# Two graph layers on one core: layer 1's sums moved next to the products of heads 0 to 3, the next tile's mask moved two steps later

## The chip, the cores and the metric

The kernel runs on one core of a Trainium2 chip. The core has a matrix engine (TensorE, PE in the profile, with its weight loads as PEld), a vector engine (VectorE, DVE), a scalar engine (ScalarE, ACT), a general one (GpSimd, POOL) and a queue engine (SyncE, SP) that issues transfers. Each works through its own instructions in order; semaphores tie them together. The metric is the time of one execution on the device in microseconds. The kernel before takes 3070.12 us, the median of three runs (3068.62 to 3073.23).

## The reference

`x` is (16, 1024, 256) in float32, `adj` (16, 1024, 1024) in int32, 0 or 1 with a full diagonal, about one entry in 32 set. Two layers follow each other, both with a normalization first and a residual:

```python
h = maximum(layernorm(x), 0)                       # layer 0: attention with 8 heads of 32
Q, K, V = (h @ W.T + bias for W, bias in ...)      # each split into heads
scores = where(adj == 0, -inf, Q @ K.T * 32**-0.5)
x = x + (softmax(scores) @ V) @ Wo.T + bo

h = maximum(layernorm(x), 0)                       # layer 1: scores by the kind of edge
e_k = leaky_relu((h * a_k) @ h.T, 0.2)             # k = 0..3
scores = where(adj == k + 1, e_k, ...)             # -9e15 where adj is 0
x = x + softmax(scores) @ h
```

With `adj` of 0 and 1, only `e_0` is ever chosen in layer 1; the kernel computes that case and looks at the end whether another kind was seen.

## The kernel before, in words

A *tile* is 128 rows of one of the 16 graphs; a graph has eight (`t` = 0 to 7), so there are 128 tiles. One loop (`for s in range(B * NT + 1)`) runs over them, and in its iteration `s` several tiles are at different stages:

- `now` is tile `s` (class `Attend`): its scores and softmax are made, head by head. `was` is tile `s - 1`: its last two heads, its products, output and residual. `gone` is tile `s - 2`, `nxt` is tile `s + 1`.
- `edge` and `edge_was` are tiles `s - 9` and `s - 10` of layer 1 (class `Edges`): scores and softmax of the one, sums and store of the other. They exist from `s` = 9 and 10 on. The last nine tiles' sums come after the loop.
- `piece` is tile `s + 9` (class `Piece`): its rows are normalized, transposed and projected to q, k and v. It exists up to `s` = 118.

Each iteration has eight *steps*, `h` = 0 to 7, one for each head. The order of the work on every engine is the order of the calls in this loop, written out by hand (`tc.manual_schedule()`); a framework sets the semaphores from the tiles that the instructions read and write. In step `h` the scores of head `h` go to one of two places of 1024 columns (`sides`; heads 4 and 6 to the second, all others to the first, since layer 1 uses the second in steps 0 to 3). DVE adds the mask and finds the row's maximum (`softmax_max`, L473), ACT takes the exponential of the head before (`softmax_exp`, L490), and the head before that is transposed: heads 0, 1, 4 and 5 by DVE in blocks and four transfers from SP (`turn_blocks`, `place_blocks`, L381 and L386), heads 2, 3, 6 and 7 by eight TensorE transposes and two ACT copies (`turn`, L590 and L591). Of tiles with `t` = 7 heads 4 and 5, and of those with `t` = 0 heads 0 and 1, go to TensorE too, with DVE copies; their exponentials write their output in another order.

Four places of 256 columns lie in two banks of the accumulation memory (shown as `acc`): `sums_place` and `brief` in the first, `early` and `late` in the second.

The work that the change touches:

- `combine(0)` in step 7 and `combine(1)` in step 3 of the next iteration: 64 products each (L526), weights of 32 columns, into `sums_place`, four of them beside each other in the array.
- `gather(0)` and `gather(1)`: layer 1's sums, 32 matmuls each (L698), also with 32 columns of weights, 256 columns moving, into `sums_place`. Half 0 ends step 5, half 1 stands in step 6 between the scores and the maximum; `store` behind the maximum divides, adds the residual (L705, L707 on DVE) and issues the output's transfer from SP (L708).
- `residual` of `was` (L547, DVE) reads the output's products (`output`, L541) from `late`; `norms` then takes the statistics of two tiles on DVE (L182, L183) and finishes them on POOL (L167 to L172). Both stand in step 5 ahead of head 5's maximum.
- `piece.turn` in step 5 writes two transposes (L237) to `late`; `piece.turned` copies them out twice on ACT (L249 `hT`, L250 `hTm`); `piece.project(0, ...)`, k's projection, ends step 6: eight matmuls (L267) to `late`; `piece.raised(0)` reads them on ACT in step 7 (L309). q's projection goes to `early` in step 1 and is read in step 4 by `raised(1)` (L309 too); `piece.normed` (L223) follows.
- `nxt.flag` on ACT (L453, squares of `adj - 0.5` with a running sum, in which other kinds of edges show) and `nxt.mask` on POOL (L441) end step 3; both write the mask of the next tile, and the one comes after the other. `nxt2.load` ends step 4: it issues, from POOL, the 512 KB load of the `adj` of the tile after that (L432), into a single buffer that flag and mask must have read.
- On POOL also: `edge.leak` (L674 to L676) and `load_nodes` (L686) in step 3, the split of q and its two transfers in step 4 (L313, L314, L324), `edge_nxt.prepare` (L613), `now.load_nodes` in step 6 (L438), the split of k in step 0.

Of the kernel before, what the change touches and what calls it, by code (L numbers as in the profile page):

```python
# [47 lines left out]
def gnn_kernel(  # L48
# [545 lines left out]
    class Edges:  # L594


        def __init__(self, b, t, last=False):
            self.b, self.t, self.last = b, t, last
            self.rows = slice(t * P, (t + 1) * P)
            self.side = sides[t % 2 if last else 1]  # L600
            self.tags = {"sel": ("p", 4), "pT1": ("pT", 7)} if last else {}
            if last and t % 2:
                self.tags |= {"ha": ("hT", 1), "x1b": ("x1", 1), "h0": ("xb", 1)}
            self.sums = late if last and t % 2 else sums_place

        def buffer(self, tag, shape):
            tag, bufs = self.tags.get(tag, (tag, 1))
# [179 lines left out]
    with tc.manual_schedule():  # L787
        first = [Piece(0, 0, 4), Piece(0, 4, 4)]
        piece_was, piece_next = Piece(1, 0), piece_of(0)
        now, nxt = attend_of(0), attend_of(1)  # L790
# [48 lines left out]
        for s in range(B * NT + 1):  # L839
            b, t = divmod(s, NT)  # L840

            def load_keys(h, end):
                if t == NT - 1 and b + 1 < B and 2 * h + end in KEY_STEPS:
                    load_key(b + 1, KEY_STEPS.index(2 * h + end))
                if t == 0 and 0 < b < B and 2 * (HEADS + h) + end in KEY_STEPS:
                    load_key(b, KEY_STEPS.index(2 * (HEADS + h) + end))

            nxt2, edge_nxt, piece_nxt = attend_of(s + 2), edges_of(s + 1), piece_of(s + 1)
            for h in range(HEADS):
                ending, eh = (now, h - 1) if h >= 1 else (was, HEADS - 1)  # L850
                turning, th = (now, h - 2) if h >= 2 else (was, HEADS + h - 2)

                load_keys(h, 0)


                if now:
                    now.scores(h)
                if h == 0 and piece_was:
                    piece_was.halve(0)
                if s == 0 and h == 1:  # L860
                    first[1].values()
                if h == 3 and edge:
                    edge.softmax_max()
                if h == 5:
                    if was:
                        was.residual()
                    norms(was, piece_nxt)
                if h == 6 and edge_was:
                    edge_was.gather(1)
                if now:  # L870
                    now.softmax_max(h)
                if h == 6 and edge_was:
                    edge_was.store()


                if h == 1 and edge:
                    edge.keep(0)
                if h == 2 and gone:
                    gone.turned_normed()
                if ending:  # L880
                    ending.softmax_exp(eh)

                if h == 3 and was:
                    was.turned_reciprocals()
                if h == 3 and edge:
                    edge.bend()
                    edge.keep(1)


                if h == 3:  # L890
                    if was:
                        was.combine(1)
                    if piece_was:
                        piece_was.biased()
                    if was:
                        was.combined()
                if turning and th in by_blocks(turning.t):
                    turning.turn_blocks(th)
                    turning.place_blocks(th)
                elif turning:  # L900
                    turning.turn(th, 0)
                    turning.turn(th, 1)


                if h == 0:
                    if edge:
                        edge.score(0)
                    if gone:
                        gone.normed()
                    if edge_was:  # L910
                        edge_was.turn_blocks()
                        edge_was.place_blocks()
                if h == 1:
                    if gone:
                        gone.turn_normed()
                    if piece_was:
                        piece_was.project(1, 0)
                        piece_was.project(1, 1)
                    if was:
                        was.reciprocals()  # L920
                    if piece_nxt:
                        piece_nxt.load()
                if h == 2:
                    if edge:
                        edge.score(1)
                    if piece_was:
                        piece_was.values()
                    if was:
                        was.turn_reciprocals()
                        was.add_bias()  # L930
                if h == 3:
                    if nxt:
                        nxt.load_queries()
                    if edge:
                        edge.leak()
                    if edge_was:
                        edge_was.load_nodes()
                    if nxt:
                        nxt.flag()
                        nxt.mask()  # L940
                if h == 4:
                    if was:
                        was.output()
                    if piece_was:
                        piece_was.raised(1)
                        piece_was.halve(1)
                    if piece:
                        piece.normed()
                    if piece_was:
                        piece_was.write_queries()  # L950
                    if edge_nxt:
                        edge_nxt.prepare()
                    if nxt2:
                        nxt2.load()
                if h == 5:
                    if edge_was:
                        edge_was.gather(0)
                    if piece:
                        piece.turn()
                    if piece:  # L960
                        piece.turned()
                if h == 6:
                    if edge:
                        edge.softmax_exp()
                    if was:
                        was.keep()
                    if now:
                        now.load_nodes()
                    if piece:
                        piece.project(0, 0)  # L970
                        piece.project(0, 1)
                if h == 7:
                    if now:
                        now.combine(0)
                    if piece:
                        piece.raised(0)
                load_keys(h, 1)
            gone, was, now, nxt = was, now, nxt, nxt2
            edge_was, edge = edge, edge_nxt
            piece_was, piece = piece, piece_nxt  # L980
# [84 lines left out]
```

## Time and profile before

| what | value |
|---|---|
| median of three runs | 3070.12 us |
| the profiled execution, its own time | 3076.4 us |
| span of its profile | 3074.5 us |
| mean granted TensorE clock | 0.996 |
| ACT, mean of 1024 exponentials (L490) | 1224 ns, and 202 ns for reading the sum |
| DVE, mean of 1024 maxima (L473) | 1208 ns, and 83 ns for reading the result |
| TensorE, layer 1's sums (L698), 8192 matmuls | 496.9 us busy |
| TensorE, the products (L526), 16384 matmuls | 533.4 us busy |
| POOL, mean of 128 masks (L441) | 3655 ns |
| ACT, mean of 128 flags (L453) | 1154 ns, and 196 ns for reading the sum |
| SP and POOL, transfers of `adj` (L432), to landing | 5.0 us |

Busy times of the engines overlap, so they do not add up to the span. A matmul's end is modelled, and matmuls overlap each other; the distance from one start to the next says what a row of them costs. In the timeline a line is a run of like instructions, with its start and its length from the first start to the last end; "idle before" in brackets gives the time that the engine stood still ahead of it and what ended it.

### The profile page before, as it was taken

How to read it: one execution, taken by the hardware profiler on the slowest of the kernel's cores; microseconds unless marked ns; L12 is line 12 of the kernel's file. 1: busy time of each engine (PE TensorE's matmuls, PEld its weight loads, DVE VectorE, ACT ScalarE, POOL GpSimd, SP SyncE). 2: the span in 40 equal slices, each digit the busy share in tenths (PEclk: the TensorE clock that was granted, in tenths of full speed). 3: DMA queues.
4: the chain of work that ended last, by engine and by line, in shares of the span. 5: the costliest groups of instructions: out<-in, count | busy, mean ns of one | idle time of the engine just before them, and what ended most of it. 6: DMA issues, size and time to landing. Idle time of an engine off the chain costs nothing. (4 is left out here: it accounts for less than half of the span.)

```text
span 3074.5 us, 96254 instructions
## 1 busy us (share of the span) xinstructions
PE 2965.6 (96%) x36722; PEld 2230.1 (73%) x36722; DVE 2515.6 (82%) x4453; ACT 2654.5 (86%) x5159; POOL 2177.6 (71%) x2999
## 2 busy tenths in 40 slices
PE   7889999999999999999999999999999999999998
PEld 5667777777777777777777777777777777776664
DVE  5878888888888888888888788888888888888885
ACT  5888888899898998889889888988989888898882
POOL 3657777777777777777777777777777777776542
PEclk9999999999999999999999999999999999999999
DMA  7766777877777786777777777787777777777653
GB/s 245 219 219 205 237 235 222 255 216 243 231 225 243 230 257 209 232 247 220 246 230 228 235 232 243 221 255 221 220 247 228 251 211 235 237 227 236 191 168 100
DMA packets 597828, 695.68 MB, mean 226 GB/s; under 512 B 63280, under 2 KB 528560, under 8 KB 597360
## 3 DMA queue, kind: packets, MB, share of 16 engines
q1 hardware_dynamic: 528288, 477.29, 51.9%
q0 software_dynamic: 66960, 210.04, 21.0%
q8 instruction: 295, 4.83, 0.7%
q10 hardware_dynamic: 2112, 2.10, 0.2%
q14 instruction: 173, 1.42, 0.1%
HBM read 252.98 MB, written 134.22 MB: 126 GB/s over the span
## 5 line engine op out<-in xcount | busy, mean ns | idle before, releaser
L473 DVE CUSTOM_DVE_ANT_0 p<-s,neg 128x1024 f32<-128x1024 f32 x1024 | 1236.2, 1208 | 220.7 <-PE s L461 185.1
L490 ACT ACTIVATE p<-p,nmx 128x1024 f32<-128x1024 f32 x1024 | 1249.4, 1224 | 132.5 <-DVE nmx L473 123.9
L461 PE MATMUL s<-k,qt 128*128 128x512 f32 x2048 | 760.6, 453 | 15.5 <-DVE nmx L473 4.3
L591 ACT COPY pT<-trp 128x512 f32<-128x512 f32 x1024 | 549.4, 590 | 95.3 <-PE trp L590 94.9
L590 PE MATMUL trp<-ident,p 128*128 128x128 f32 x4608 | 604.5, 274 | 4.7 <-ACT pT L591 1.5
L590 PEld LDWEIGHTS trp<-ident,p 128*128 128x128 f32 x4608 | 531.0, 140 | 104.0 <-ACT pT L591 10.8
L381 DVE STREAM_TRANSPOSE blocks<-p 128x1024 f32<-128x1024 f32 x456 | 564.5, 1238 | 12.3 <-ACT p L680 10.6
L526 PE MATMUL acc<-pT,v 128*32 128x128 f32 x16384 | 533.4, 275 | 41.8 <-ACT recT L520 30.0
L526 PEld LDWEIGHTS acc<-pT,v 128*32 128x32 f32 x16384 | 453.5, 110 | 153.0 <-ACT recT L520 85.0
L698 PE MATMUL acc<-h,pT 128*32 128x256 f32 x8192 | 496.9, 382 | 2.8 <-DVE h L707 1.7
L441 POOL TENSOR_SCALAR neg<-adj 128x1024 bf16<-128x1024 int32 x128 | 467.9, 3655 | 42.9 <-ACT neg L453 33.7
L461 PEld LDWEIGHTS s<-k,qt 128*128 128x128 f32 x2048 | 322.9, 191 | 106.3 <-issue 43.0
L698 PEld LDWEIGHTS acc<-h,pT 128*32 128x32 f32 x8192 | 241.8, 109 | 207.8 <-issue 65.6
L676 POOL TENSOR_TENSOR sel<-sel,less 128x1024 f32<-128x1024 f32 x120 | 286.8, 2390 | 68.9 <-ACT less L665 47.6
L633 PE MATMUL s<-h1T,ha 128*128 128x512 f32 (+2 forms) x744 | 272.8, 490 | 2.7 <-ACT h1T L569 1.6
L674 POOL TENSOR_SCALAR less<-top 128x1 f32<-128x1 f32 x120 | 31.9, 266 | 274.0 <-DVE top L656 273.9
L324 POOL DMA_DIRECT2D qd<-halves x240 | 177.5, 780 | 58.7 <-POOL halves L314 31.8
L490 ACT ACTIVATION_READ_ACCUMULATOR p<-p,nmx 128x1 f32 x1024 | 206.8, 202 | 0.0
L510 POOL COPY wide<-rec 128x256 f32<-128x256 f32 x128 | 53.8, 420 | 204.2 <-DVE rec L508 204.2
L330 POOL DMA_DIRECT2D kd<-halves x240 | 172.2, 766 | 35.5 <-POOL halves L314 35.4
L314 POOL TENSOR_TENSOR halves<-full,halves 128x256 fp32r<-128x256 f32 x240 | 176.8, 737 | 20.6
L633 PEld LDWEIGHTS s<-h1T,ha 128*128 128x128 f32 x744 | 126.7, 190 | 70.7 <-issue 45.0
(117 smaller groups left out, 4328.4 us busy)
## 6 DMA issues: line engine op xcount, KB each, us to landing
pT<-blocks SPq DMA_DIRECT2D x2304, 128.0 KB, 3.5
qt<-qd SPq DMA_DIRECT2D x128, 512.0 KB, 4.5
k<-kd SPq DMA_DIRECT2D x128, 512.0 KB, 7.3
adj<-in_adj POOLq DMA_DIRECT2D x127, 512.0 KB, 5.0
qd<-halves POOLq DMA_DIRECT2D x240, 256.0 KB, 2.7
kd<-halves POOLq DMA_DIRECT2D x240, 128.0 KB, 4.1
xb<-in_x POOLq DMA_DIRECT2D x128, 128.0 KB, 4.2
x1d<-x SPq DMA_DIRECT2D x128, 128.0 KB, 4.0
```

The source lines that it names most:

```text
L324: nc.gpsimd.dma_start(out=qds[self.b][self.first, oc].rearrange("p u w n -> p u (w n)"), in_=halves.unsqueeze(1).to_broadcast([P, 2, 2 * P]),)
L381: nc.vector.transpose(blocks.rearrange("p b j q -> p j b q"), p)
L441: nc.gpsimd.tensor_scalar(self.neg, self.adj, 0.0, MASKED, ALU.is_equal, ALU.mult)
L461: nc.tensor.matmul(self.ps[:, cols], lhsT=self.qt[:, h, :], rhs=keysets[self.b][h][:, cols], start=True, stop=True,)
L473: nc.vector.tensor_tensor_reduce(out=p, in0=sides[h in self.second], in1=self.neg, scale=-SCALE, scalar=FLOOR, op0=ALU.add, op1=ALU.min, a ...
L490: nc.scalar.activation(to, of, AF.Exp, bias=nmx, scale=-1.0, accum_out=self.sums[:, h : h + 1])
L526: nc.tensor.matmul(sums_place[r * HD : (r + 1) * HD, g * P : (g + 1) * P], lhsT=vs[self.b][:, j, place_of(h) : place_of(h) + HD], rhs=self ...
L590: nc.tensor.transpose(tr[:, j, :], p[:, jj * P : (jj + 1) * P], ident)
L591: copy(pT[:, half * 4 : half * 4 + 4, :], tr)
L633: nc.tensor.matmul(self.side[:, cols], lhsT=self.ha[:, c, :], rhs=h1T[:, c, cols], start=(c == 0), stop=(c == NC - 1),)
L676: nc.gpsimd.tensor_tensor(self.sel, self.sel, self.less, ALU.subtract)
L698: nc.tensor.matmul(self.sums[a * HD : (a + 1) * HD, :], lhsT=self.pT[:, j, a], rhs=h1s[self.b][:, j, :], start=(j == 0), stop=(j == NT - 1),)
```

## The change

In the loop, five moves; in `Edges.__init__` one place. Layer 1's two half sums and the store leave steps 5 and 6 and stand in step 7 between k's projection, which leaves the end of step 6, and `combine(0)`; inside the loop they use `early` in place of `sums_place`. The maximum of a head is now called ahead of the residual and the norms for all heads (it matters in step 5 alone). Flag and mask of the next tile go from the end of step 3 to the end of step 5, the load of `adj` from the end of step 4 to the start of the second half of step 6. Nothing is added to or taken from the instructions themselves.

```diff
-            self.sums = late if last and t % 2 else sums_place
+            self.sums = (late if t % 2 else sums_place) if last else early
...
                 if h == 3 and edge:
                     edge.softmax_max()
+                if now:
+                    now.softmax_max(h)
                 if h == 5:
                     if was:
                         was.residual()
                     norms(was, piece_nxt)
-                if h == 6 and edge_was:
-                    edge_was.gather(1)
-                if now:
-                    now.softmax_max(h)
-                if h == 6 and edge_was:
-                    edge_was.store()
...
                     if edge_was:
                         edge_was.load_nodes()
-                    if nxt:
-                        nxt.flag()
-                        nxt.mask()
                 if h == 4:
...
                     if edge_nxt:
                         edge_nxt.prepare()
-                    if nxt2:
-                        nxt2.load()
                 if h == 5:
-                    if edge_was:
-                        edge_was.gather(0)
                     if piece:
                         piece.turn()
                     if piece:
                         piece.turned()
+                    if nxt:
+                        nxt.flag()
+                        nxt.mask()
                 if h == 6:
+                    if nxt2:
+                        nxt2.load()
                     if edge:
                         edge.softmax_exp()
...
                     if now:
                         now.load_nodes()
+                if h == 7:
                     if piece:
                         piece.project(0, 0)
                         piece.project(0, 1)
-                if h == 7:
+                    if edge_was:
+                        edge_was.gather(0)
+                        edge_was.gather(1)
+                        edge_was.store()
                     if now:
                         now.combine(0)
```

## The prediction

> **What bounds the kernel now.** I read the busy shares of the page first, then one query tile's period on each engine's timeline, then a few windows. Three engines are near full on the page, and TensorE is fullest:
>
> ```profile
> PE 2965.6 (96%) x36722; PEld 2230.1 (73%) x36722; DVE 2515.6 (82%) x4453; ACT 2654.5 (86%) x5159; POOL 2177.6 (71%) x2999
> ```
>
> A share does not say who sets the pace, so I took TensorE's timeline of one tile, from the scores of head 4 to those of head 0 of the next tile (columns: start, duration, engine, line, what, count):
>
> ```profile
> 1638.65 0.73 PE L461 MATMUL s<-k,qt 128*128 128x512 f32 x2
> ...
> 1640.77 0.81 PE L461 MATMUL s<-k,qt 128*128 128x512 f32 x2
> 1641.42 1.03 PE L590 MATMUL trp<-ident,p 128*128 128x128 f32 x8
> 1642.39 1.93 PE L698 MATMUL acc<-h,pT 128*32 128x256 f32 x32
> 1644.25 0.44 PE L237 MATMUL acc<-ident,h 128*128 128x128 f32 x2
> 1644.45 0.71 PE L461 MATMUL s<-k,qt 128*128 128x512 f32 x2
> 1645.09 1.93 PE L698 MATMUL acc<-h,pT 128*32 128x256 f32 x32
> 1646.96 1.16 PE L267 MATMUL acc<-hT,wkT 128*128 128x128 f32 x8
> 1647.87 0.71 PE L461 MATMUL s<-k,qt 128*128 128x512 f32 x2
> 1648.52 1.96 PE L526 MATMUL acc<-pT,v 128*32 128x128 f32 x64
> 1650.40 0.73 PE L461 MATMUL s<-k,qt 128*128 128x512 f32 x2
> ```
>
> No line shows an idle time, and the stretch is 11.75 us long. I tabulated it over 78 tiles with t from 1 to 6: it lies between 11.73 and 11.76 in every one. So steps 4 to 7 are set by TensorE alone, and that is where the change works. The other engines of the same stretch:
>
> ```profile
> 1642.14 0.42 DVE L547 TENSOR_TENSOR x<-acc,xb 128x256 f32<-128x256 f32 x1 [0.58 <-issue]
> ...
> 1645.20 1.23 DVE L473 CUSTOM_DVE_ANT_0 p<-s,neg 128x1024 f32<-128x1024 f32 x1 [0.32 <-PE s L461]
> ```
>
> ```profile
> 1641.41 0.64 ACT L309 ACTIVATE full<-acc,bq_t 128x128 f32<-128x128 f32 x2
> 1641.92 0.62 ACT L223 ACTIVATE h<-xin,shift,r 128x256 f32<-128x256 f32 x1
> 1642.41 1.16 ACT L490 ACTIVATE p<-p,nmx 128x1024 f32<-128x1024 f32 x1
> 1643.54 1.09 ACT L591 COPY pT<-trp 128x512 f32<-128x512 f32 x2
> 1644.73 0.37 ACT L249 COPY hT<-acc 128x256 f32<-128x256 f32 x1
> 1645.00 0.38 ACT L250 COPY hTm<-acc 128x256 f32<-128x256 f32 x1
> ```
>
> The reader is to see that ACT runs from 1641.41 on with almost no gap, that hTm is done at 1645.38, only 1.6 us before its reader L267, and that the residual L547 stands ahead of head 5's maximum (1643.68, not shown). The two half sums (L698) are what covers these two. In all tiles L547 starts 0.09 us after the second L309 ends or later: both read the bank acc1, one after the other.
>
> **The change on TensorE: what it removes.** Sums between full-array work cost more than their matmuls. The 32 of a half start 1.55 us from first to last (1.93 less one matmul of 0.38), 0.05 each, so 1.60 by themselves, but stand 1.86 to 1.87 apart from what follows: 0.27 to leave. Entering costs 0.09 (transposes to sums 0.97, to L541 0.88; scores to sums 0.64, to transposes 0.57). L267 behind them needs 0.91, elsewhere 0.82. Now the 64 stand in one row with heads 0 to 3's products, both 128x32: one entry, no exit of their own. Step by step, the new row without any wait would be transposes 0.88, L237 0.20, scores 0.56, scores 0.56, L267 0.82 with 0.09 to enter, sums 64 x 0.05 = 3.20, products 1.88: 8.19 instead of 1650.40 - 1641.42 = 8.98. Gain: 0.79 us a tile.
>
> **What the change adds on the path: two waits.** The diff moves head 5's maximum ahead of the residual and the statistics in step 5; only one call moved, but on DVE's queue it changes who waits. L237 writes the place that the residual reads (`late`), so it can't start before it, and the 1.95 us of sums that lay between are gone.
> (a) Head 5's scores end at 1641.58, the maximum starts 0.04 later (as at 1645.20, behind scores that end at 1645.16) and gives DVE free after 1.15; the residual runs 1642.77 to 1643.19; L237 at about 1643.25 (0.06 is what the scores of head 1 need behind a maximum). TensorE is ready at 1641.42 + 0.88 = 1642.30. Wait 0.95.
> (b) L237 0.20, scores 0.56 twice: L267 could start at 1644.57. It needs hTm. ACT without the flag in step 3 starts L309 as soon as the output's products end (1641.13, plus 0.1, which is where L309 stands in the tiles in which ACT is early: 2.57 us after head 4's scores): 1641.22. Then, by the starts above, 0.51 + 0.49 + 1.13, then 0.95 for the copies (1503.81 to 1504.76 in a tile with t = 7), 0.27 and 0.38: hTm at 1644.95. L267 0.07 later, 1645.02. Wait 0.45. So the flag, gone from step 3, buys only 0.2 us here, since ACT then waits for TensorE.
> Sum for a tile: 0.95 + 0.45 - 0.79 = **0.61 us slower**; heads 0 to 3 end at 1651.01.
>
> **Tiles with t = 7** take a third wait. There heads 4 and 5 are transposed on TensorE in steps 6 and 7, and their exponentials, which reorder, take twice as long:
>
> ```profile
> 1505.28 2.26 ACT L490 ACTIVATE p<-p,nmx 128x1024 f32<-128x1024 f32 x1
> ```
>
> That is head 5's, right behind hTm; the next ACT work starts 2.07 later. The flag (L453: 1.15 from its start, 1638.18, to the next) now sits ahead of it: 1505.28 + 1.15 + 2.07 = 1508.50. Head 5's transposes start at 1508.6; TensorE, without the sums before it, is through with head 7's scores near 1506 and waits 2.6 us. Then 0.85 + 0.91 + 3.20 + 1.88 = 1515.4, against 1511.57 before: 3.87 slower.
>
> **A wait also costs clock.** Of the first ten tiles six have a stretch of 3.41 us at half clock, each behind a 3.41 us stretch with 1.69 us or more of idle TensorE; stretches with 1.64 or less did not have it:
>
> ```profile
> 57.66:61.07 3.41, 1.33 (x8) 0.87 (x8) 2.77 (x5) 3.41 (x8) 2.96 (x5) 1.00 0.00 0
> 61.07:64.48 3.41, 3.41 (x33) 2.67 (x36) 1.58 (x4) 2.34 (x6) 3.08 (x8) 0.50 0.76 238
> ```
>
> (PE busy is the first number after the length, the granted clock the third from the end.) The price, from the starts in that tile: L267 to scores 1.40 for 0.91, scores to products 1.13 for 0.65, products 2.48 for 1.88, 1.6 in all. A wait of 2.6 reaches 1.69 in one of two stretches about 8 times in 10. The waits of the other tiles leave TensorE idle for some 1.1 to 1.4 us within one stretch, so none is taken there; at the upper end one tile in six.
> The Trainium skill ("TensorE: Matmul & The Clock Gate", Part 1 and its closing table) asks for an idle window or gap of about 3.4 us before the clock is halved. By that rule a wait of 2.6 us costs no clock and the forecast would be 17 us lower; the rows above show it behind 1.7 us, and I go by them.
>
> **What lies beside other work.** The mask (3.66 us) moves on POOL behind the split of q, its two DMAs, the scaling of the next tile and the norms. POOL by its rows: split from 1641.95, DMAs from 1643.0, scaling 1644.75, norms 1645.7 to 1647.35, mask to 1651.0. Its reader, head 0's maximum of the next tile, waits for scores that end at 1651.87 then: margin 0.85, price nothing; beyond it each us would be paid in full. The load of adj (0.80 to issue, 5.0 to land) is issued at 1651 and needed a period later. On DVE the store waits for the sums (end 1649.5) with nothing behind it but that same maximum; its DMA passes two heads' block moves on SP's queue and has only layer 1's next blocks behind it, which need DVE first. k's evacuation on ACT (L309) now stands behind the store, in one bank, until 1650.5; head 7's exponential is then done near 1651.7, and its transposes come after the next scores of head 1. Head 5's exponential, behind the flag in the other tiles too, ends at 1647.1, and DVE comes to its transposes at 1647.7. All at nothing.
>
> **Sum.** Sums in the loop from s = 10, a piece to project until s = 118: 109 tiles, 13 of them with t = 7. 96 x 0.61 = 59; 13 x 3.87 = 50; clock 13 x 0.8 x 1.6 = 17; s = 119, t = 7 without a piece, +3; the last nine tiles have no piece, hence no wait (a) or (b), and DVE and ACT take part of the gain: -4 (between 0 and -7). The first ten have no sums: 0 (5 either way). Together +125: the profiled span 3074.5 (run 3076.4) becomes 3200; against the median 3070.1, **3195 us**.
>
> **Rivals.**
> 1. The waits stay hidden and the gain is kept. For it: TensorE is the full engine, and 0.79 is solid. It needs (a) and (b) to add to less than 0.79, that is the residual done 0.6 us earlier than DVE's own rows allow. 119 x -0.79 = -94: 2976. Chance 0.04.
> 2. Only (a) binds because ACT is early by half a us, and the flag does not delay head 5: 109 x 0.16 = 17: 3087. Against it: the copies' durations are fixed and their start is set by TensorE. Chance 0.06.
> 3. The mask comes late on POOL. Its margin is 0.85 us; at 1.85 us of delay, from a slower split or contention, a us more on each of 109 tiles: 3304. Chance 0.06.
> 4. The two orders are the same in effect: no change, 3070. Against it: the instruction listings differ as described. Chance 0.02.
>
> The likeliest has 0.82. Range 3140 to 3230: the low end is (a) and (b) together 0.25 shorter, t = 7 at 2.5 and no clock lost (96 x 0.36 + 13 x 2.5 = 67); the high end has 0.15 more a tile and the clock lost in one tile of six (14 + 25). A difference over 0.2% (6 us) can be told from none here: faster 0.04, same 0.02, slower 0.94.
>
> **What would show it.** Right: in the changed trace L237 waits about 0.9 us for DVE's L547, L267 some 0.4 for ACT's L250, the 64 sums run straight into the 64 products, head 4's scores to head 0's take 12.3 us (17 or more for t = 7), and the clock falls in the t = 7 tiles. Wrong: L237 without idle time; head 0's maximum waiting for POOL's L441; or a gap between the sums and the products.

## The result, and the profile after

| | median | lowest to highest | runs |
|---|---|---|---|
| before | 3071.68 us | 3068.62 to 3074.89 | 4 |
| changed | 3241.62 us | 3240.40 to 3244.79 | 4 |

The changed kernel takes 1.0555 times as long, with a 95% interval of 1.0536 to 1.0573: 170 us slower. The forecast was 3195 us within 3140 to 3230. The sign and the causes were right; the amount was 45 us short, and 12 us outside the range. The span of the changed kernel's profile is 3238.5 us against 3074.5, so 164 us have to be found in the trace.

The busy shares of the page first. TensorE does the same 36722 matmuls in nearly the same busy time as before, but the share is 91% instead of 96%: it now waits.

```profile
PE 2954.5 (91%) x36722; PEld 2278.3 (70%) x36722; DVE 2506.4 (77%) x4453; ACT 2661.5 (82%) x5159; POOL 2178.2 (67%) x2999
```

The view of waits says for what. Its columns are the engine with its line, the work it waited for, the total in us, how often, and the longest; three lines of the changed kernel:

```profile
PE acc L237 <- DVE x L547: 104.1, 118, 1.0
...
PE trp L590 <- ACT p L490: 40.1, 18, 2.6
...
PE acc L267 <- ACT hTm L250: 37.7, 106, 1.3
```

These are the forecast's three waits: the transposes of the piece for the residual, head 5's transposes in the tiles with `t` = 7, and k's projection for the second copy. TensorE's timeline of one regular tile, from head 4's scores to the next head 0's, shows where two of them stand:

```profile
1683.23 0.73 PE L461 MATMUL s<-k,qt 128*128 128x512 f32 x2
...
1685.35 0.81 PE L461 MATMUL s<-k,qt 128*128 128x512 f32 x2
1686.00 1.03 PE L590 MATMUL trp<-ident,p 128*128 128x128 f32 x8
1687.99 0.41 PE L237 MATMUL acc<-ident,h 128*128 128x128 f32 x2 [0.96 <-DVE x L547]
1688.16 1.18 PE L461 MATMUL s<-k,qt 128*128 128x512 f32 x4
1689.60 1.16 PE L267 MATMUL acc<-hT,wkT 128*128 128x128 f32 x8 [0.26 <-ACT hTm L250]
1690.69 3.66 PE L698 MATMUL acc<-h,pT 128*32 128x256 f32 x64
1694.17 1.93 PE L526 MATMUL acc<-pT,v 128*32 128x128 f32 x64
1696.03 0.73 PE L461 MATMUL s<-k,qt 128*128 128x512 f32 x2
```

The two that TensorE waited for, on DVE and on ACT:

```profile
1686.28 1.22 DVE L473 CUSTOM_DVE_ANT_0 p<-s,neg 128x1024 f32<-128x1024 f32 x1
...
1687.43 0.42 DVE L547 TENSOR_TENSOR x<-acc,xb 128x256 f32<-128x256 f32 x1
```

```profile
1688.88 0.40 ACT L249 COPY hT<-acc 128x256 f32<-128x256 f32 x1
1689.14 0.41 ACT L250 COPY hTm<-acc 128x256 f32<-128x256 f32 x1
```

The residual starts when head 5's maximum is through, ends at 1687.85, and L237 follows 0.14 later. The copies end at 1689.55, and L267 follows 0.05 later. In this tile the two idle times are 0.96 and 0.26; their medians over the regular tiles are 0.88 and 0.34. The stretch is 12.80 us, where it was 11.75; I tabulated it for every tile, and 12.80 is the median of the 83 regular ones (`t` = 1 to 6, `s` = 10 to 118).

So the 164 us of span come from these places. Each sum is the stretch after less the stretch before, added up over the tiles; the columns between show medians, or the range:

| tiles | stretch before | after | sum |
|---|---|---|---|
| 83 with `t` = 1 to 6 | 11.74 | 12.80 | +87.6 us |
| 13 with `t` = 0 | 12.14 | 13.19 | +13.6 us |
| 13 with `t` = 7 | 13.44 | 17.63 to 19.28 | +68.7 us |
| `s` = 119, `t` = 7 without a piece | 12.64 | 17.34 | +4.7 us |
| `s` = 120 to 126 | 11.16 | 10.27 | -5.9 us |
| everything else: the first ten tiles, steps 0 to 3, the end | | | -5 us |

### The profile page after: what moved, and what is told of

Read it like the earlier page. It is cut to its first block, busy times and chain, and to the rows that moved or that the text cites. A ratio compares the mean times of both kernels' runs of the same rounds, so it can differ in the third digit from the quotient of the medians.

```text
span 3238.5 us, 95849 instructions
## 1 busy us (share of the span) xinstructions
PE 2954.5 (91%) x36722; PEld 2278.3 (70%) x36722; DVE 2506.4 (77%) x4453; ACT 2661.5 (82%) x5159; POOL 2178.2 (67%) x2999
## 5 line engine op out<-in xcount | busy, mean ns | idle before, releaser
L461 PE MATMUL s<-k,qt 128*128 128x512 f32 x2048 | 730.2, 446 | 24.7 <-DVE nmx L473 14.6
L590 PE MATMUL trp<-ident,p 128*128 128x128 f32 x4608 | 612.6, 276 | 55.2 <-ACT p L490 40.1
L526 PE MATMUL acc<-pT,v 128*32 128x128 f32 x16384 | 523.3, 274 | 26.7 <-ACT recT L520 23.7
L526 PEld LDWEIGHTS acc<-pT,v 128*32 128x32 f32 x16384 | 462.9, 110 | 109.9 <-ACT recT L520 78.7
L698 PE MATMUL acc<-h,pT 128*32 128x256 f32 x8192 | 475.2, 382 | 2.0 <-DMA pT<-blocks 1.2
L698 PEld LDWEIGHTS acc<-h,pT 128*32 128x32 f32 x8192 | 256.5, 110 | 181.4 <-issue 6.5
L313 POOL CAST halves<-full 128x256 fp32r<-128x256 f32 x240 | 96.8, 403 | 233.1 <-ACT full L309 233.1
L324 POOL DMA_DIRECT2D qd<-halves x240 | 173.5, 774 | 58.7 <-POOL halves L314 31.8
L309 ACT ACTIVATE full<-acc,bk_t 128x128 f32<-128x128 f32 x240 | 75.2, 366 | 161.5 <-DVE h L707 159.2
```

Of the source, the lines that this page charges most:

```text
L461: nc.tensor.matmul(self.ps[:, cols], lhsT=self.qt[:, h, :], rhs=keysets[self.b][h][:, cols], start=True, stop=True,)
L526: nc.tensor.matmul(sums_place[r * HD : (r + 1) * HD, g * P : (g + 1) * P], lhsT=vs[self.b][:, j, place_of(h) : place_of(h) + HD], rhs=self ...
L590: nc.tensor.transpose(tr[:, j, :], p[:, jj * P : (jj + 1) * P], ident)
L698: nc.tensor.matmul(self.sums[a * HD : (a + 1) * HD, :], lhsT=self.pT[:, j, a], rhs=h1s[self.b][:, j, :], start=(j == 0), stop=(j == NT - 1),)
```

## The experiments

Each kernel was run beside the kernel before on one chip; the kernel before had medians from 3069.10 to 3072.73 us there, so the kernels can also be held against each other. "Stretch" is always from head 4's scores to the next head 0's, and positions are counted in us from head 4's scores.

**The residual ahead of the maximum again.** Is wait (a) there because the maximum now stands ahead of the residual, and what does it cost?

```diff
+                if h == 5:
+                    if was:
+                        was.residual()
+                    norms(was, piece_nxt)
                 if now:
                     now.softmax_max(h)
-                if h == 5:
-                    if was:
-                        was.residual()
-                    norms(was, piece_nxt)
```

> The changed kernel with one thing undone: in step 5 the residual and the statistics stand ahead of head 5's maximum again. Theory (two waits, each behind its own engine): wait (a) of L237 shrinks from 1.0 to about 0.1 us, but the maximum now ends 1.8 us later, at 6.0 us after head 4's scores, and head 7's scores, in the same place as head 5's, wait for it; k's projection L267 moves from 6.37 to 6.65. So 0.28 us slower on 96 tiles, nothing at t = 7: about +27 us against the changed kernel, 3268. Rival (the order of maximum and residual is the fault): L267 comes earlier by the part of (a) that (b) does not cover, 0.4 us or more on 109 tiles, 3200 or less.

It took 3262.39 us (3258.60 to 3268.12), 1.0621 [1.0593, 1.0648] of before. L237 starts 3.85 after head 4's scores instead of 4.69, as early as said, but L267 at 6.65 instead of 6.37, and the stretch is 12.98 at the median: slower. TensorE's timeline of one tile, from head 6's scores on:

```profile
1525.40 0.71 PE L461 MATMUL s<-k,qt 128*128 128x512 f32 x2
1527.46 0.73 PE L461 MATMUL s<-k,qt 128*128 128x512 f32 x2 [1.35 <-DVE nmx L473]
1528.04 1.06 PE L267 MATMUL acc<-hT,wkT 128*128 128x128 f32 x8
1529.02 3.66 PE L698 MATMUL acc<-h,pT 128*32 128x256 f32 x64
```

The residual first releases the transposes, but residual and statistics now delay head 5's maximum on DVE. Head 7's scores go to the place that this maximum reads and wait for it: they start 6.09 behind head 4's scores, where they start at 5.40 in the changed kernel, and L267 stands directly behind them without a wait. The copies on ACT are not what holds it: `hTm` starts at 5.92, and at 5.91 in the changed kernel. This is the theory as written. Wait (a) was no loss that could be taken back by itself, and the diff's order is the better one here.

**Flag, mask and load back in steps 3 and 4.** What do the moves that have nothing to do with the sums bring?

```diff
                 if h == 3:
...
+                    if nxt:
+                        nxt.flag()
+                        nxt.mask()
...
                 if h == 4:
...
+                    if nxt2:
+                        nxt2.load()
                 if h == 5:
...
-                    if nxt:
-                        nxt.flag()
-                        nxt.mask()
                 if h == 6:
-                    if nxt2:
-                        nxt2.load()
```

> The changed kernel with flag, mask and load of adj back in steps 3 and 4. Theory: at t = 7 head 5's exponential starts 1.15 earlier, so head 5's transposes come at 9.3 instead of 10.4 us after head 4's scores and the wait is mostly too short to halve the clock: 13 x 1.1 + some 10 to 14 us. In the other tiles ACT is later by the flag again, q's evacuation L309 starts 2.57 to 2.97 instead of 2.57, and L267 comes 0.2 later on average: +20. The masks that came late (12 tiles at 0.7) are early again: -9. In all -5 to -20 us: 3220 to 3237. Rival (the flag ahead of head 5's exponential is the main cost in all tiles): under 3190.

3226.84 us (3223.41 to 3228.37), 1.05 [1.0476, 1.0524]: within the range given. The stretches with `t` = 7 are mostly 16.85 to 17.1 instead of 17.63 and more, and no head 0 of the 109 tiles has its maximum more than 0.91 behind its scores; the regular tiles lose 0.3 (13.10), since ACT has the flag ahead of the copies again: the first copy starts at 5.94 instead of 5.65. So the move of flag, mask and load, on top of the others, costs 15 of the 170 us; the other 155 belong to the moves of the sums, of k's projection and of the maximum.

**The piece's transposes in another bank.** Wait (a) is a wait for a place. With `brief` in place of `late`, L237 needs the residual no more:

```diff
-                    tr = by_chunk(late)
+                    tr = by_chunk(brief)
```

> The changed kernel with the transposes L237 in the place brief of the first bank, so that they need not wait for the residual. Theory: wait (a) is gone, L237 starts at 3.64 instead of 4.69 us after head 4's scores, but hTm is set by ACT's own row (copies end at 5.65) and L267 stays at 6.37: wait (b) grows to about 1.3 us, no change in time, 3241 within 8. Rival (the residual alone sets L237 and what follows): the 1.0 us comes back on 109 tiles, about 3140.

3216.26 us (3211.90 to 3216.89), 1.0466 [1.0441, 1.0490]: 25 us faster than the changed kernel where the expectation was no change. L237 starts at 3.74, near the 3.64 expected. The expectation's error was L267, which I took to be bound at 6.37 by the copies whatever L237 does. TensorE's timeline:

```profile
1502.75 1.03 PE L590 MATMUL trp<-ident,p 128*128 128x128 f32 x8
1503.71 0.44 PE L237 MATMUL acc<-ident,h 128*128 128x128 f32 x2
1503.90 1.16 PE L461 MATMUL s<-k,qt 128*128 128x512 f32 x4
1506.07 1.16 PE L267 MATMUL acc<-hT,wkT 128*128 128x128 f32 x8 [1.01 <-ACT hT L249]
```

The bracket now names L249, the first copy, and not L250. k's projection reads `hT` alone (the prediction had "It needs hTm"), and `hTm` held it up only because its result went to the place out of which the second copy still read. Apart, it starts one copy earlier, at 6.10, and the stretch is 12.52. The wait of 1.01 that is left is that of ACT's queue.

**The sums ahead of k's projection.** The order in step 7 turned round, so that the sums cover the copies:

```diff
-                    if piece:
-                        piece.project(0, 0)
-                        piece.project(0, 1)
                     if edge_was:
                         edge_was.gather(0)
                         edge_was.gather(1)
                         edge_was.store()
+                    if piece:
+                        piece.project(0, 0)
+                        piece.project(0, 1)
```

> The changed kernel with the sums ahead of k's projection in step 7, so that 3.3 us of work cover ACT's copies. Theory: wait (b) of 0.42 us goes, an exit from the sums (0.27) and a second entry come: head 4's scores to the next head 0's 12.5 instead of 12.8 us in tiles with t from 1 to 6, L267 without a wait; about -25 us, 3216. Rival (L267's delay is not ACT but the row of matmuls itself): no gain, and 0.3 us a tile more for the second entry, 3270.

3354.80 us (3353.34 to 3360.51), 1.0923 [1.0896, 1.0951]: 113 slower than the changed kernel, against both expectations. TensorE's timeline:

```profile
1520.88 1.18 PE L461 MATMUL s<-k,qt 128*128 128x512 f32 x4
1522.40 3.66 PE L698 MATMUL acc<-h,pT 128*32 128x256 f32 x64 [0.34 <-ACT hTm L250]
1527.01 1.16 PE L267 MATMUL acc<-hT,wkT 128*128 128x128 f32 x8 [0.94 <-DVE h L707]
1528.09 1.96 PE L526 MATMUL acc<-pT,v 128*32 128x128 f32 x64
```

The sums read nothing that the copies write. They wait for them because `early`, where the sums go, lies in one bank with `late`, out of which the copies read; and k's projection, into `late`, waits for DVE's store, which reads `early`. So in this kernel the accesses of two engines to one bank come one after the other, whatever part of it they touch. (The program declares each bank as one tile, and `early` and `late` are its two halves; whether the order comes from the tile or from the bank itself no run tells apart.) This agrees with the Trainium skill ("PSUM — Partial Sum Buffer", the section on bank collisions), which asks for semaphores by bank, or bank and quadrant, and not by address. Here the price was 0.34 and 0.94 us in this tile, and the stretch is 1.15 longer than the changed kernel's (13.95).

**An order by banks.** From that follows an order that goes from one of the two banks to the other and back: transposes to `brief`; sums to `early` right behind head 7's scores (head 6's where `t` = 7), by which time residual and q's evacuation are done with that bank; heads 0 to 3; and k's projection last, when the store has read `early`. k's evacuation moves to step 0 of the next iteration. Flag, mask and load stay where they were before. Against the kernel before:

```diff
-                    tr = by_chunk(late)
+                    tr = by_chunk(brief)
...
-            self.sums = late if last and t % 2 else sums_place
+            self.sums = (late if t % 2 else sums_place) if last else early
...
-        piece_was.raised(0)
...
-                if h == 0 and piece_was:
-                    piece_was.halve(0)
...
-                if h == 5:
-                    if was:
-                        was.residual()
-                    norms(was, piece_nxt)
-                if h == 6 and edge_was:
-                    edge_was.gather(1)
+                if h == (6 if t == 7 else 7) and edge_was:
+                    edge_was.gather(0)
+                    edge_was.gather(1)
                 if now:
                     now.softmax_max(h)
-                if h == 6 and edge_was:
+                if h == 7 and edge_was:
                     edge_was.store()
+                if h == 5:
+                    if was:
+                        was.residual()
+                    norms(was, piece_nxt)
...
                     ending.softmax_exp(eh)
+                if h == 0 and piece_was:
+                    piece_was.raised(0)
+                    piece_was.halve(0)
...
                 if h == 5:
-                    if edge_was:
-                        edge_was.gather(0)
...
-                    if piece:
-                        piece.project(0, 0)
-                        piece.project(0, 1)
                 if h == 7:
                     if now:
                         now.combine(0)
                     if piece:
-                        piece.raised(0)
+                        piece.project(0, 0)
+                        piece.project(0, 1)
```

> A version that keeps the row of sums and the early maximum of the change, and takes away what waits: piece's transposes L237 in brief (first bank), sums right behind head 7's scores (behind head 6's at t = 7), the store behind head 7's maximum, then the products of heads 0 to 3, then k's projection, whose evacuation L309 stands in step 0 behind head 7's exponential; flag, mask and load of adj where they were before the change. Theory (the bank that residual, copies, sums and k's projection share makes the waits): nothing waits in steps 5 to 7; after head 4's scores L237 at 3.73, sums at 5.1, products at 8.6, k's projection at 10.5, the next head 0's scores at 11.4 against 11.74 in the kernel before and 12.8 in the changed one; t = 7 at 13.3 against 13.44: about -40 us against before, 3030. Rival (the row of sums brings nothing, only waits were moved): 3070 or more.

3033.99 us (3029.41 to 3039.53), 0.9877 [0.9856, 0.9898] of before: faster than both, and near the 3030 expected. The regular stretches lie between 11.29 and 11.70, those with `t` = 7 between 13.61 and 13.95, above the 13.3 expected and above before. Not all of the gain is the row's: of the 41 us of span, 11.6 come from the stretches of the first ten tiles, which have no sums. Neither L267 nor the sums have an idle time ahead of them. In this order the row without waits is worth 0.44 us a tile in the shortest stretches (11.74 less 11.30), not 0.79.

**The same with flag, mask and load as in the diff.** This puts the mask's delay by itself on an otherwise tight kernel:

> As the version before, but with flag, mask and load of adj in steps 5 and 6 as in the change. Theory: the period is now so short that the mask on POOL, done some 12.4 us after head 4's scores, comes after the next scores of head 0 (ready at 12.3): head 0's maximum waits 0.1 to 0.4 us for it in each tile, and at t = 7 head 5's transposes wait 0.8 us for their exponential: 10 to 50 us slower than the version with the flag in step 3, 3040 to 3080. Rival (place of the mask indifferent): the same time within 8 us.

```diff
                 if h == 3:
...
-                    if nxt:
-                        nxt.flag()
-                        nxt.mask()
...
-                    if nxt2:
-                        nxt2.load()
...
                     if piece:
                         piece.turned()
+                    if nxt:
+                        nxt.flag()
+                        nxt.mask()
                 if h == 6:
+                    if nxt2:
+                        nxt2.load()
```

3104.22 us (3102.44 to 3107.20), 1.0107 [1.0090, 1.0124]: 70 slower than without, more than said. The mask on POOL and the maximum on DVE that waits for it, of one tile:

```profile
1459.20 3.65 POOL L441 TENSOR_SCALAR neg<-adj 128x1024 bf16<-128x1024 int32 x1
```

```profile
1462.89 1.23 DVE L473 CUSTOM_DVE_ANT_0 p<-s,neg 128x1024 f32<-128x1024 f32 x1 [1.84 <-POOL neg L441]
```

Head 0's scores start at 1461.40; the maximum could follow 0.86 after them and follows 1.49 after. The view of waits gives that wait 206.0 us in 101 tiles, where the changed kernel has 52.1 in 22, and steps 0 to 3, in which head 0's maximum stands, take 66.5 us more than in the version without the moved flag. This is rival 3's mechanism. In the changed kernel it hardly shows: the two other waits make the stretch 1.5 longer (12.80 against 11.31), and at the median the mask is done 0.11 before the scores of head 0 start, where here it is done 1.43 after they start.

**The same with L237 in `late`.** Is it the place of the transposes that decides?

```diff
-                    tr = by_chunk(brief)
+                    tr = by_chunk(late)
```

> As the first of this call, but the transposes L237 in late again, the bank of the sums. Theory: L237 waits for the residual (4.7 instead of 3.73), and the sums, in the same bank, wait for both copies on ACT (6.5 instead of 5.1, at t = 7 some 2.7 us later): 1.4 us on 96 tiles, 2.7 on 13, 170 us slower than the first: 3200. Rival (only the order on the queues counts, not the bank): the same time as the first within 10 us.

3203.20 us (3199.91 to 3204.18), 1.0429 [1.0412, 1.0446]: as said. One word costs 169 us: L237 starts at 4.69 again, and the sums at 6.4 to 6.8, behind the copies' reads of their bank.

**The sums alone.** The kernel before, with sums and store in step 7 and in `early`, and nothing else moved:

```diff
-            self.sums = late if last and t % 2 else sums_place
+            self.sums = (late if t % 2 else sums_place) if last else early
...
-                if h == 6 and edge_was:
-                    edge_was.gather(1)
                 if now:
                     now.softmax_max(h)
-                if h == 6 and edge_was:
-                    edge_was.store()
...
-                    if edge_was:
-                        edge_was.gather(0)
...
                 if h == 7:
+                    if edge_was:
+                        edge_was.gather(0)
+                        edge_was.gather(1)
+                        edge_was.store()
                     if now:
                         now.combine(0)
```

> The kernel before with one part of the change alone: sums and store in step 7 ahead of the products, in early; k's projection, maximum and residual, flag, mask and load as before. Theory: the sums had covered the wait for the copies; L267, still ahead of head 7's scores, waits for hTm until 6.6, head 7's scores 7.4, sums 8.1, products 11.6, next head 0's scores 13.4: 1.7 us slower on 96 tiles, some 2.3 at t = 7, 3250 to 3270, slower than the whole change. Rival (grouping the sums is a gain, the other moves are what costs): below 3070.

3299.09 us (3291.29 to 3302.97), 1.0744 [1.0726, 1.0762]: slower than the whole change, as said, and some 30 us more than said. Most stretches are 13.26 to 13.67, where I had worked out 13.4; but 15 of the 83 are about 15. One of these, on TensorE's timeline and in four half microseconds (columns of the latter: length, busy time of PE, PEld, DVE, ACT and POOL, then the granted clock and the DMA share and rate):

```profile
1339.26 1.63 PE L267 MATMUL acc<-hT,wkT 128*128 128x128 f32 x8 [1.64 <-ACT hTm L250]
1340.55 1.20 PE L461 MATMUL s<-k,qt 128*128 128x512 f32 x2
1341.68 4.38 PE L698 MATMUL acc<-h,pT 128*32 128x256 f32 x64
```

```profile
1339.00:1339.50 0.50, 0.24 (x2) 0.24 (x3) 0.50 (x1) 0.50 (x2) 0.41 (x2) 1.00 0.78 221
...
1340.00:1340.50 0.50, 0.50 (x5) 0.50 (x4) 0.50 (x3) 0.50 (x3) 0.32 (x1) 0.50 1.07 323
...
1342.50:1343.00 0.50, 0.50 (x12) 0.23 (x8) 0.50 (x3) 0.10 (x2) 0.50 (x2) 0.50 0.99 367
...
1343.50:1344.00 0.50, 0.50 (x16) 0.29 (x12) 0.50 (x1) 0.00 (x0) 0.47 (x1) 1.00 0.98 201
```

Behind a wait of 1.64 us, with one of 0.34 us shortly before it, the clock is halved for some 3.4 us. Such waits don't do it each time: of the 54 regular tiles with 1.6 or more ahead of L267 and 0.3 or more ahead of L237, 8 lose clock and 46 keep it. The trace shows what differs. The stretches at half clock start whole multiples of 3.413 us apart, so they lie on a fixed beat, and it counts how much idle time falls into one beat: 1.68 us or more in all 25 beats behind which the clock fell, and at most 1.80 in those behind which it stayed (counted from 20 us after the start). In the changed kernel k's projection stands one row of scores later, in step 7, and its wait is 0.26 to 0.35 (0.61 in one tile).

**The normalized rows first.** In the version ordered by banks (the expectation speaks of three; they are the two banks, used in turn) L237 starts between 3.75 and 4.15, since L223, whose rows it transposes, stands behind q's evacuation on ACT. Turned round:

```diff
+                    if piece:
+                        piece.normed()
                     if piece_was:
                         piece_was.raised(1)
                         piece_was.halve(1)
-                    if piece:
-                        piece.normed()
```

> This is the version with the three banks apart, and in step 4 the normalized rows (L223) ahead of q's evacuation (L309) on ACT. In that version the two transposes L237 start between 3.75 and 4.14 us after head 4's scores; 3.75 is where TensorE alone puts them, and what they lie beyond it adds up to 25 us over the 109 tiles, since they wait for L223 there. Theory: with L223 first they start at 3.75 in every tile, and each stretch from head 4's scores to the next head 0's is 11.30 to 11.35 (t = 1 to 6): 3034 - 25 = 3009, between 3003 and 3017. Rival: the start of L237 decides nothing, because what follows it is bound by q's evacuation, which now comes half a us later (the sums write the place that it reads): then L237 starts at 3.75, the sums still at 5.3 and more, and the time stays at 3034, within 6.

3012.06 us (3011.02 to 3020.77), 0.9806 [0.9791, 0.9821] of before: as said, and the fastest kernel of this study. L237 starts at 3.64 and the median stretch is 11.18, shorter than said; steps 0 to 3 take 10 us more in sum, so the total agrees in part by luck. TensorE's timeline, to be held against the one of the changed kernel:

```profile
1381.15 1.03 PE L590 MATMUL trp<-ident,p 128*128 128x128 f32 x8
1382.02 0.38 PE L237 MATMUL acc<-ident,h 128*128 128x128 f32 x2
1382.16 1.21 PE L461 MATMUL s<-k,qt 128*128 128x512 f32 x4
1383.30 3.66 PE L698 MATMUL acc<-h,pT 128*32 128x256 f32 x64
1386.78 1.93 PE L526 MATMUL acc<-pT,v 128*32 128x128 f32 x64
1388.63 1.16 PE L267 MATMUL acc<-hT,wkT 128*128 128x128 f32 x8
1389.55 0.71 PE L461 MATMUL s<-k,qt 128*128 128x512 f32 x2
```

No bracket in it: TensorE is fed without a gap, with the sums and the products still in one row.

**The sums twice.** What does a row of sums cost? The changed kernel, with the whole sum computed a second time in place of the first:

```diff
                     if edge_was:
                         edge_was.gather(0)
                         edge_was.gather(1)
+                        edge_was.gather(0)
+                        edge_was.gather(1)
                         edge_was.store()
```

> The changed kernel with layer 1's sums computed twice over in step 7, the second time in place of the first: 64 matmuls of 128x32 more in the row, nothing else. Theory: four matmuls start together and such a group costs 0.2175 us, so the row of 128 takes 32 x 0.2175 = 6.96 from its first start to the products, a regular tile's stretch is 12.80 + 3.48 = 16.28, and the whole 3242 + 109 x 3.48 = 3621. Rival, the prediction's 0.05 for each matmul: 3.48 as measured and 3.20 more, 6.68, a stretch of 16.00, and 3590. A fixed 0.28 to begin the row and 0.05 each, which the 3.48 of 64 alone can't tell from the first theory, gives the rival's numbers too: the added 64 decide.

One run, 3648.41 us, beside 3069.1 for the kernel before. The row, and what follows it:

```profile
1662.56 7.11 PE L698 MATMUL acc<-h,pT 128*32 128x256 f32 x128
1669.49 1.93 PE L526 MATMUL acc<-pT,v 128*32 128x128 f32 x64
1671.35 0.73 PE L461 MATMUL s<-k,qt 128*128 128x512 f32 x2
```

1669.49 - 1662.56 = 6.93 from the first start to the products, against 3.48 for 64 (1694.17 - 1690.69); the median over the tiles is 6.93 too. So the added 64 cost 3.45, which is 16 groups of four at 0.2156: the theory's 3.48 within 0.03, and not the prediction's 3.20. The regular stretch is 16.25 (theory 16.28, rival 16.00). The whole is 27 us above the theory's figure, which counted 109 tiles; the sums also run in the loop's last tiles, and `s` = 119 to 126 add 27.4 us in the trace.

## Why the prediction was right, and where it failed

Its steps for a regular tile can be laid beside the trace, as positions from head 4's scores:

| start of | forecast | median measured |
|---|---|---|
| the piece's transposes L237 | 4.60 | 4.69 |
| k's projection L267 | 6.37 | 6.37 |
| the sums L698 | 7.28 | 7.46 |
| the products L526 | 10.48 | 10.94 |
| the next head 0's scores | 12.36 | 12.80 |

- **Waits (a) and (b)** were right in cause and nearly in size: the forecast had 0.95 and 0.45, the trace shows 0.88 and 0.34 as idle time at the median. By their effect they are 0.95 (L237 starts at 4.69, and at 3.74 with its transposes in the other bank) and 0.40 (L267 follows the scores before it by 0.97, and by 0.57 where it has no wait, as with the residual first). L267 came out where it was put, because its start is set by the end of the copies. That it waits for the second copy is due to the place of its result, not to its input, which is the first.
- **The gain of 0.79 is the step that failed.** All of the miss, 12.80 - 12.36 = 0.44, lies behind L267. Of this 0.28 is the row of sums, 3.48 instead of 64 x 0.05 = 3.20, the rest lies between L267 and the sums. The prediction read 0.05 out of the first and last start of 32 matmuls, 1.55 apart. But four of them start within 0.02, and the groups of four follow each other by 0.2175: eight groups have first starts 7 x 0.2175 = 1.52 apart and take 1.74, not 1.60. What the prediction had booked as 0.27 "to leave" the row, and as saved by the change, was by this reckoning 0.13 to leave and 0.14 of sums that stay. The row computed twice shows it directly, and the profile of before could have: it has rows of 64 behind the loop, whose first and last start are 3.28 apart, 1.73 more for 32 more matmuls.
- That rest is 0.18: 1.09 from L267 to the sums instead of 0.91. The version with the residual first splits it. There L267 stands between the same neighbours without a wait, in 82 of the 83 regular tiles, and 0.98 separates it from the sums. So 0.10 comes with the wait: the eight matmuls of L267 have first and last start 0.88 apart behind it, and 0.78 without. The other 0.08 is the entry into the row of sums, put at 0.09: the last of the eight starts 0.20 ahead of the sums, and 0.03 ahead of scores where these follow, 0.17 less.
- 96 tiles x 0.44 = 42 us, and 125 + 42 = 167 of the 170. So no large wait was overlooked, and the range's high end was missed by the mis-sized gain. (That end was 3230 by its text; its own terms, 14 and 25 us on 3195, give 3234.) With the row at 3.48 the forecast would have been 109 x 0.28 = 31 higher, 3226 us.
- **The tiles with `t` = 7** came out near the forecast in sum, 68.7 us against 13 x 3.87 + 17 = 67, in part by luck. One that lost clock and one that kept it, each with the idle stretch and the one behind it; of the first also TensorE's timeline:

```profile
1585.73 0.71 PE L461 MATMUL s<-k,qt 128*128 128x512 f32 x2
1589.02 1.66 PE L590 MATMUL trp<-ident,p 128*128 128x128 f32 x8 [2.58 <-ACT p L490]
1590.47 1.92 PE L267 MATMUL acc<-hT,wkT 128*128 128x128 f32 x8
```

```profile
1586.00:1589.40 3.40, 0.82 (x5) 0.39 (x5) 1.96 (x4) 3.40 (x5) 3.07 (x5) 1.00 1.01 321
1589.40:1592.80 3.40, 3.40 (x23) 2.95 (x25) 1.45 (x3) 1.78 (x4) 3.10 (x3) 0.50 1.01 404
...
794.10:797.51 3.41, 1.61 (x10) 1.11 (x10) 3.35 (x6) 3.41 (x7) 2.99 (x8) 1.00 0.86 278
797.51:800.92 3.41, 2.39 (x27) 2.10 (x31) 1.36 (x3) 3.17 (x6) 3.33 (x1) 1.00 1.02 402
```

- The wait was forecast as 2.6 and is 2.58. The clock falls to 0.50 behind a stretch with 2.58 idle out of 3.40: 9 of the 13 tiles take 19.0 to 19.3 instead of 17.6 to 17.9, where 8 times in 10 and 1.6 us were forecast. Two small errors offset each other: at full clock these tiles lost 4.2 to 4.5, not 3.87 (0.28 of it is the row of sums again), and fewer of them lost clock. The limit of 1.69, read from the first tiles of before, was too low for these: the four tiles that kept the clock had 1.8 to 1.9 idle in their emptiest stretch (1.80 above), the nine that lost it 2.0 or more. The rows of before gave the price; the rule of 3.4 us of idle time (the Trainium skill, "TensorE: Matmul & The Clock Gate", Part 1) would have had no tile at half clock.
- **Rival 1** (waits hidden) and **rival 2** (only one wait) are out by the waits. **Rival 4** is out. **Rival 3** was real and small: head 0's maximum starts more than 1.1 us behind its scores in 12 of the 109 tiles. Eleven of these lie nine or eighteen tiles apart (`s` = 11 to 110): there q's transfer on POOL (L324) starts some 2.08 us behind the split instead of 0.30, and the mask comes 1.8 later. What holds the transfer in every ninth tile is not shown. In sum over the 109 tiles, steps 0 to 3 are 5.8 us shorter than before all the same. The margin of 0.85 that held the rival off was the longer stretch itself, as the version ordered by banks shows with the moved flag (70 us slower than without).
- Work taken at nothing stayed at nothing: k's evacuation waits up to 6.0 us for the store, 159.2 in sum, and nothing in the stretch waits for it.

Why then does a change that takes rows out of TensorE's way lose? It took 1.95 us of sums from between the residual and the piece's transposes, and as much from between these and k's projection. By the forecast's sizes the two waits cost 1.40 a tile, and the rest of the change then brought 0.79 - 0.44 = 0.35, which gives the measured 1.05. The version ordered by banks keeps the one row and puts it between the transposes and k's projection again, and there the gain is kept.

## What to carry to other kernels

Before two rows are put next to each other, ask what the moved one was hiding, and give the next pair of dependent steps another cover. Take the price of a row of narrow matmuls from its length as a whole, from its first start to the start of what follows, in two lengths of the row: the distance of first and last start leaves out the last group of matmuls that start together. And where two engines take turns on one bank, the place of a result decides as much as the order: one name changed moved 169 us.

## What the runs showed of the hardware

- Four 128x32 matmuls beside each other in the array, 256 columns moving, in float32: the four start within 0.02 us, and groups follow each other by 0.2156 to 0.2175 us. A row of 16 groups takes 3.48 us, one of 32 groups 6.93. Entering such a row behind full-array matmuls costs 0.17 us more than going on with these (0.20 against 0.03 behind the last start of L267).
- The half clock comes in stretches of 3.413 us, which start whole multiples of 3.413 us apart within a trace, and it follows a stretch of that beat with much idle TensorE. In the changed kernel it fell behind 1.96 to 2.59 us of idle time and not behind 1.91 or less; with the sums alone it fell behind 1.68 to 2.06 and not behind 1.67 or less, while stretches with 1.68 to 1.80 went either way. The same pair of waits, 1.64 and 0.34, lost clock in some tiles and kept it in others. In the changed kernel's regular tiles 0.88 and 0.34 within 2.6 us did not halve it.
- Eight full-array matmuls (L267) have their first and last start 0.78 us apart right behind scores, and 0.88 behind a wait or behind a row of narrow matmuls.
